# Projections in fours, one evacuation of two value banks, earlier expert rows and a spaced closing in a conv, attention and mixture-of-experts kernel

## The chip, the cores and the metric

The kernel runs on one core of a Trainium2 chip. The metric is the device time of one execution in microseconds; the time before is 1307.98 us, the median of 3 runs (1307.3 to 1308.54). A profiled execution takes longer: the one shown here ran 1332.96 us, and its trace spans 1331.2 us, with a mean granted TensorE clock of 0.989.

Engines are named as the profile names them: PE (TensorE, matmuls), PEld (its weight loads), DVE (VectorE), ACT (ScalarE), POOL (GpSimd) and SP (SyncE, which issues most DMAs). Every engine takes its own instructions in program order.

## The reference

The input is two images of 256 channels and 56 x 56 = 3136 positions, all in float32. Two layers follow each other:

```python
# layer 0: non-local block, 8 groups of 16 channels, no softmax
f = einsum('bgdn,bgdm->bgnm', theta(x), phi(x)) / n
y = einsum('bgnm,bgdm->bgdn', f, g(x))
x = relu(batch_norm(w_out @ y + b_out) + x)

# layer 1: tokens t of shape (2, 3136, 256)
q, k, v = split(ln(t) @ W_attn)                 # 4 heads of 64, causal softmax
t = t + (softmax(mask(q @ k.T / 8)) @ v) @ W_proj
probs = softmax(ln(t) @ gate_w + gate_b)        # 8 experts, each token takes 2
t = t + sum over the 2 experts of p_e * (gelu(ln(t) @ W1[e] + b1[e]) @ W2[e] + b2[e])
```

The output is t, brought back to the image layout.

## The kernel before

The kernel folds layer 0 into one matrix per image, then runs attention image by image (b = 0, 1), and then the experts. Tokens are sorted by expert into blocks of 128 rows ("slots") in DRAM, so each block is a small dense network. The engines' program order is written by hand. Background work is kept in generators, and a part of it is emitted ("pulled") between attention steps or expert blocks.

Attention goes over seven query blocks of W = 448 columns, two pairs of heads (hp) and key tiles of 128. One step is one `scores` and one `values`, three steps apart. The matmuls work on 64x64 tiles of the array, four at a time:

```python
LAG = 3
for n in range(len(steps) + LAG):
    if n < len(steps):
        ...
        between(i, ends[i] - n)             # background work of this step
    late = n >= LAG and steps[n - LAG][3]   # first values of a block
    if n >= LAG:
        due(clock[0])                       # tasks whose time has come
        clock[0] += 1
    if n >= LAG and not late:
        values(n - LAG)
    if n < len(steps):
        scores(n)
    if late:
        values(n - LAG)
```

`scores` writes exponentials into a tile `st` (a pool of 5), and DVE adds them into `acc`, for the softmax's sums:

```python
nc.scalar.activation(st[:k, :, c0:], ps[:k, :, c0:W], AF.Exp, scale=SCALE)    # L661
...
nc.vector.tensor_tensor(acc, acc, st, ALU.add)                                # L675
```

`values` accumulates into two PSUM banks, one for each half of a key tile's 128 rows. The tile that holds them, `yp`, has one buffer (`py`, bufs=1). At the end of a block both banks are brought out and added:

```python
if last:
    yh = qT[:, hp, i * W : (i + 1) * W]
    nc.scalar.copy(yh, yp[:, 0, :W])                              # L703
    nc.vector.tensor_tensor(yh, yh, yp[:, 1, :W], ALU.add)        # L704
    later.append((clock[0], sum_rows, hp, i, yh))
```

Then come, by the clock, `sum_rows` (a matmul with ones, a copy, four small DMAs and a fifth), `invert` (a reciprocal on DVE, L740, and three DMAs), `scale` (a product on DVE) and `hand_on`. For the last block of all, the DMAs of these go through POOL's queue (`queue_of`).

The projections of the next tokens are cut into pieces: a Q or K piece is a 512-column product for one pair of heads (L539), a V piece is one token tile (L558), and a transpose piece (L518) makes two token tiles ready. Each writes a PSUM bank of a pool with two buffers (`pm`, tag "m"), which ACT then copies out. They use the whole 128x128 array. They are emitted by `between`:

```python
tick[0] += 1
if tick[0] % 2:
    pull(2)
    return
nb, s = (b, i + 1) if i + 1 < NB else (b + 1, 0)
if nb < B and s < NS and (nb == b or left < NCH - QB // P - 2):
    rest = max(0, upto[s] - at[nb] - 1)
    for _ in range(2 * -(-rest // max(2, left))):
        if at[nb] + 1 < upto[s]:
            step(nb)
```

After attention the experts run block by block, GB = 3 blocks to a group. The first group's rows are brought in during attention (`early_rows`); later groups are fetched six blocks ahead. For each block PE transposes the rows (L1380), multiplies them by the first weights (L1403) and, three blocks later, by the second (L1422). DVE copies the block's first weights out of the resident ones two blocks ahead (L1391) and adds the second bias (L1432). Between blocks, `meanwhile` pulls the background work; first in that queue is `closing`, which finishes the last attention block:

```python
def closing():
    while finished[B - 1][NH - 1] < N:
        clock[0] += 4
        due(clock[0])
        yield True
        yield True
    while not projected[B - 1]:
        yield False
    queue.append(judge())
    ...

def meanwhile():
    scatters = placed[1] and not sent[1]
    pull(3 if scatters or worked[0] >= MIXED else 2)
    if side and next(side[0], None) is None:
        side.popleft()
```

After it, the second image's tokens are projected out, sorted (small DVE operations) and scattered to their slots (indirect DMAs of POOL), all beside the blocks of the first image.

Of the kernel before, what the change touches and what calls it, by code (L numbers as in the profile page):

```python
# [27 lines left out]
def conv_attn_moe_kernel(  # L28
# [75 lines left out]
    MIXED = MOST0 + E  # L104
    NBLK = (2 * B * N + E * (P - 1)) // P
    GB = 3

    MAIN = NBLK - GB
    SCALE = 1.0 / HS**0.5
# [333 lines left out]
    def layer1(nm, general):  # L443

        with ExitStack() as whole:
# [170 lines left out]
            def attend(  # L616
# [63 lines left out]
                def values(n):  # L680
                    i, hp, j, first, last, order = steps[n]
                    k = chunk(j)
                    c0 = max(0, j * P - i * W)
                    sn = f"{nm}{b}_{hp}_{i}"
                    st = sts.pop(n)
                    if first:
                        yps[hp, i] = py.tile([P, 2, 512], F32, tag="y", name=f"yp_{sn}")
                    yp = yps[hp, i]

                    for h in range(0, k, HS):  # L690
                        end = last or (h and all(chunk(o) <= h for o in order[order.index(j) + 1 :]))
                        for a in range(2):
                            nc.tensor.matmul(  # L693
                                yp[a * HS : (a + 1) * HS, h // HS, c0:W],
                                v[hp][h : h + HS, j, a, :HS],
                                st[h : h + HS, a, c0:],
                                start=first,
                                stop=bool(end),
                            )
                    if last:  # L700

                        yh = qT[:, hp, i * W : (i + 1) * W]
                        nc.scalar.copy(yh, yp[:, 0, :W])  # L703
                        nc.vector.tensor_tensor(yh, yh, yp[:, 1, :W], ALU.add)  # L704
                        del yps[hp, i]
                        later.append((clock[0], sum_rows, hp, i, yh))

                def queue_of(hp, i):

                    return nc.gpsimd if (b, hp, i) == (B - 1, NH - 1, NB - 1) else nc.sync  # L710

                def sum_rows(hp, i, yh):
                    r = (b * NH + hp) * NB + i
                    sn = f"{nm}{b}_{hp}_{i}"
                    acc = accs.pop((hp, i))
                    sp = bank(f"sp_{b}_{hp}_{i}")

                    flat = acc.rearrange("p a w -> p (a w)")
                    for g in range(4):
                        nc.tensor.matmul(  # L720
                            sp[g * 32 : (g + 1) * 32, : W // 2], ones[:, :32],
                            flat[:, g * W // 2 : (g + 1) * W // 2], start=True, stop=True,
                        )
                    line = fs.tile([P, W], F32, tag="rb", bufs=3, name=f"line_{sn}")
                    nc.scalar.copy(line[:, : W // 2], sp[:, : W // 2])
                    halves = sum_d[r].rearrange("a (h w) -> (a h) w", h=2)
                    for g in range(4):
                        queue_of(hp, i).dma_start(
                            out=halves[g : g + 1], in_=line[g * 32 : g * 32 + 1, : W // 2]
                        )  # L730
                    queue_of(hp, i).dma_start(
                        out=sums[:, r], in_=sum_d[r].rearrange("a (p f) -> (a p) f", p=HS)
                    )
                    later.append((clock[0] + 4, invert, hp, i, yh))

                def invert(hp, i, yh):
                    r = (b * NH + hp) * NB + i
                    sn = f"{nm}{b}_{hp}_{i}"
                    back = fs.tile([P, 2 * W // P], F32, tag="back", name=f"back_{sn}")
                    nc.vector.reciprocal(back, sums[:, r])  # L740
                    queue_of(hp, i).dma_start(
                        out=inv_d[r].rearrange("a (p f) -> (a p) f", p=HS), in_=back
                    )
                    rb = fs.tile([P, W], F32, tag="rb", bufs=3, name=f"rb_{sn}")
                    for a in range(2):
                        queue_of(hp, i).dma_start(
                            out=rb[a * HS : (a + 1) * HS], in_=inv_d[r, a].partition_broadcast(HS)
                        )
                    later.append((clock[0] + 4, lambda hp, i, yh: scale(hp, i, yh, rb), hp, i, yh))
# [551 lines left out]
            def experts(w1s, w2s, b2s, ex, es, ps6, between, need, written):  # L1301
# [4 lines left out]
                def fetch(g):  # L1306
                    s, e = g * GB, (g + 1) * GB
                    b = 0 if e <= FULL0 else 1
                    need(b)
                    if g == 0:  # L1310
                        return early_rows, None
                    f = known[b][0]
                    xb = ex.tile([P, GB, xds[b].shape[1]], F32, tag="xb", bufs=3, name=f"xb_{nm}_{g}")
                    if b:
                        at = nc.values_load_multi_w_load_instructions(
                            qblk[0:1, s - f : e - f],
                            engines=(SP,),
                            min_val=0,
                            max_val=NBLK - FULL0 - 1,
                            skip_runtime_bounds_check_because="a permutation's places",  # L1320
                        )[1]
# [52 lines left out]
                def inputs(n, group):  # L1374
                    xb, to = group
                    g = n % GB
                    rows = xb[g] if n < GB else xb[:, g, :C]
                    tp = ps6.tile([P, 512], F32, tag="tp", bufs=2, name=f"tp_{nm}_{n}")
                    for c in range(NH):
                        nc.tensor.transpose(  # L1380
# [257 lines left out]
            def tokens(b, qT, done):  # L1638
# [5 lines left out]
                if b == 0:  # L1644
# [8 lines left out]

                    while not read[B - 1]:
                        yield False
                    for n in range(0, GB, 2):
                        m = min(2, GB - n)
                        xb = bg.tile([P, 2, C], F32, tag="xn", name=f"xb_{nm}_first{n}")
                        nc.sync.dma_start(
                            out=xb[:, :m],  # L1660
                            in_=xds[0][n * P : (n + m) * P].rearrange("(n p) w -> p n w", p=P),
# [49 lines left out]
            else:  # L1711
# [27 lines left out]
                for b in range(B):  # L1739
# [5 lines left out]
                    def between(i, left):  # L1745
# [6 lines left out]
                        tick[0] += 1  # L1752
                        if tick[0] % 2:
                            pull(2)
                            return
                        nb, s = (b, i + 1) if i + 1 < NB else (b + 1, 0)

                        if nb < B and s < NS and (nb == b or left < NCH - QB // P - 2):
                            rest = max(0, upto[s] - at[nb] - 1)
                            for _ in range(2 * -(-rest // max(2, left))):  # L1760
                                if at[nb] + 1 < upto[s]:
                                    step(nb)

# [6 lines left out]
            def closing():  # L1770

                if not general:
                    while finished[B - 1][NH - 1] < N:
                        clock[0] += 4
                        due(clock[0])
                        yield True
                        yield True
                    while not projected[B - 1]:
                        yield False
                    queue.append(judge())  # L1780
# [5 lines left out]
            with ExitStack() as moe:  # L1786
# [11 lines left out]
                        )  # L1798
                for _ in load_w2(True):
                    pass  # L1800
                while len(early_rows) < GB:
                    pull()

                def need(b):
# [9 lines left out]
                    queue.appendleft(finish(1, oy, 3))  # L1814

                def meanwhile():
                    scatters = placed[1] and not sent[1]
                    pull(3 if scatters or worked[0] >= MIXED else 2)
                    if side and next(side[0], None) is None:
                        side.popleft()  # L1820

# [179 lines left out]
```

## Time and profile before

| What | us |
|---|---|
| median time | 1307.98 |
| profiled span | 1331.2 |
| PE busy | 1276.9 |
| DVE busy | 787.7 |
| ACT busy | 602.2 |
| POOL busy | 306.2 |
| last attention product ends, experts begin, about | 887 |
| last expert product ends, about | 1310.7 |

The page gives for each engine its busy time, its share of the span and its instructions. Busy time of PE is modelled from pipelined matmuls, and a float32 matmul counts as two instructions. The chain of work follows the end back, step by step, to what released it; its shares by engine say which engine set the time. A row of groups reads: line, engine, operation, tiles, shapes and count, then busy time and mean of one in ns, then the idle time just before them with what ended it. A row of waits reads: who waited, for whom, the sum in us, the number of times, the longest. A timeline row reads: start and length in us, engine, line, operation, tiles, count, and in brackets the idle time before with its releaser. Times in windows are from the span's start.

### The profile page before, as it was taken

The page shows a single profiled execution, that of the slowest core. Times are in us where ns is not written, and L with a number is a line of the kernel's source. Part 1 is how long each engine was busy: PE and PEld are TensorE (multiplying, and loading weights), DVE is VectorE, ACT ScalarE, POOL GpSimd, SP SyncE. Part 2 cuts the span into 40 slices and gives each one's busy share as a digit, 9 for nine tenths or more (in the row PEclk, how much of TensorE's full clock was granted, in tenths as well). Part 3 has the DMA queues.
Part 4 walks back from the last instruction along what each step waited for, and adds up shares of the span by engine and source line. Part 5 has one row for each costly group of instructions (what it writes and reads, how often), then busy time and mean ns, then how long its engine had stood idle before and what let it go on. Part 6 is the DMA issues. An engine that isn't in the chain of part 4 may idle for free.

```text
span 1331.2 us, 28014 instructions
## 1 busy us (share of the span) xinstructions
PE 1276.9 (96%) x10569; PEld 808.0 (61%) x10569; DVE 787.7 (59%) x1683; ACT 602.2 (45%) x1226; POOL 306.2 (23%) x297
## 2 busy tenths in 40 slices
PE   8999999999999999999999989989999999899995
PEld 7875444444444444444345434449988999899894
DVE  1582555748777654675768777765744443355553
ACT  0145554555565554455553455553423333244341
POOL 1113110000000111110004461010066212655541
PEclk9999999999999999999999999999999999999997
DMA  9993000000000000100001126141244433556553
GB/s 311 383 326 113 16 24 24 24 16 24 9 17 17 17 2 9 40 9 15 9 8 60 60 80 198 33 138 56 67 144 129 130 109 97 179 175 202 180 156 107
DMA packets 110471, 123.54 MB, mean 93 GB/s; under 512 B 19904, under 2 KB 100045, under 8 KB 110329
## 3 DMA queue, kind: packets, MB, share of 16 engines
q1 hardware_dynamic: 96232, 92.49, 22.4%
q0 software_dynamic: 10272, 26.00, 5.8%
q10 hardware_dynamic: 3824, 3.18, 0.8%
q8 instruction: 87, 1.43, 0.5%
q14 instruction: 56, 0.45, 0.1%
HBM read 62.65 MB, written 60.41 MB: 92 GB/s over the span
## 4 chain that ended last, share of the span: by engine, by line
PE 91%; DVE 3%; issue 2%; ACT 1%; DMA 1%; POOL 0%; DVEq 0%; SPq 0%; POOLq 0%; ACTq 0%
PE yp_f L693 20%; PE sc_f L653 19%; PE ht_f L1403 14%; PE yp_f L1422 13%; PE qk_f L539 7%; PE v_f L558 4%; PE pp_f L602 4%; PE cp L324 3%; PE gram L255 3%; PE tp_f L1380 2%; DVE acc_f L675 1%; ACT st_f L661 1%; PE sp_f L720 1%; PE yo_f L1549 1%; PE xp_f L518 1%
## 5 line engine op out<-in xcount | busy, mean ns | idle before, releaser
L661 ACT ACTIVATE st_f<-sc_f 128x896 f32<-128x896 f32 (+5 forms) x400 | 333.5, 838 | 300.1 <-PE sc_f L653 273.7
L675 DVE TENSOR_TENSOR acc_f<-acc_f,st_f 128x896 f32<-128x896 f32 (+5 forms) x372 | 366.5, 985 | 168.3 <-ACT st_f L661 161.3
L693 PE MATMUL yp_f<-st_f,v_f 64*64 64x448 f32 (+6 forms) x3184 | 340.5, 503 | 9.7 <-DVE qT_f L704 6.5
L653 PE MATMUL sc_f<-qT_f,kT_f 64*64 64x448 f32 (+6 forms) x3184 | 341.5, 500 | 4.0 <-ACT st_f L661 4.0
L1412 ACT ACTIVATE g_f<-ht_f,b1b 128x128 f32<-128x128 f32 x408 | 116.8, 371 | 243.0 <-PE ht_f L1403 127.6
L1403 PE MATMUL ht_f<-xT_f,w_f 128*128 128x128 f32 x1632 | 203.4, 277 | 9.3 <-issue 6.6
L653 PEld LDWEIGHTS sc_f<-qT_f,kT_f 64*64 64x64 f32 x3184 | 116.6, 133 | 156.4 <-issue 134.5
L693 PEld LDWEIGHTS yp_f<-st_f,v_f 64*64 64x64 f32 x3184 | 112.3, 133 | 162.6 <-issue 134.7
L1403 PEld LDWEIGHTS ht_f<-xT_f,w_f 128*128 128x128 f32 x1632 | 198.5, 193 | 14.9 <-issue 10.4
L501 POOL TENSOR_SCALAR xn_f<-t 128x256 f32<-128x256 f32 (+1 forms) x50 | 68.2, 1373 | 542.6 <-issue 330.8
L1284 POOL DMA_INDIRECT x_slots<-xr_f,idx x100 | 113.0, 1130 | 218.7 <-DVE xr_f L1276 116.6
L1391 DVE COPY w_f<-w1s_f 128x1024 f32 x102 | 71.1, 698 | 86.8 <-PE ht_f L1403 38.8
L539 PE MATMUL qk_f<-px_f,wat 128*128 128x512 f32 (+1 forms) x224 | 92.6, 558 | 1.2 <-ACT px_f L524 1.2
L1439 POOL DMA_INDIRECT y_tokens<-ys_f,to_f x60 | 60.3, 1005 | 139.7 <-DVE ys_f L1432 109.8
L1432 DVE TENSOR_TENSOR ys_f<-yp_f,kT_f 128x128 f32<-128x128 f32 x102 | 29.6, 291 | 99.7 <-PE yp_f L1422 65.3
L663 DVE TENSOR_TENSOR st_f<-st_f,keep 128x256 f32<-128x256 f32 (+1 forms) x112 | 44.2, 395 | 68.2 <-ACT st_f L661 67.7
L539 PEld LDWEIGHTS qk_f<-px_f,wat 128*128 128x128 f32 x224 | 38.7, 190 | 54.4 <-issue 45.3
L1422 PE MATMUL yp_f<-px_f,g_f 128*128 x204 | 62.7, 390 | 1.0 <-issue 1.0
L1422 PE MATMUL yp_f<-v_f,g_f 128*128 x204 | 61.5, 382 | 0.8 <-issue 0.8
L1422 PE MATMUL yp_f<-kT_f,g_f 128*128 x204 | 62.1, 386 | 0.0
L1422 PE MATMUL yp_f<-w2s_f,g_f 128*128 x204 | 61.2, 382 | 0.3 <-issue 0.3
L1496 POOL DMA_INDIRECT y_f<-y_slots,idx x50 | 54.8, 1096 | 16.3 <-issue 14.7
(259 smaller groups left out, 1170.8 us busy)
## 6 DMA issues: line engine op xcount, KB each, us to landing
x_slots<-fill SPq DMA_DIRECT2D x1, 8127.0 KB
xb_f<-x_slots SPq DMA_DIRECT2D x60, 129.0 KB
x_slots<-fill SPq DMA_DIRECT2D x1, 7296.0 KB
y_slots<-ys_f SPq DMA_DIRECT2D x57, 128.0 KB
kept<-t SPq DMA_DIRECT2D x2, 3200.0 KB
x<-in_x_dram SPq DMA_DIRECT2D x14, 448.0 KB
xr<-in_x_rows_dram SPq DMA_DIRECT2D x12, 512.0 KB
out_dram<-ot_f SPq DMA_DIRECT2D x24, 256.0 KB
```

Of the source, the lines that this page charges most:

```text
L501: nc.gpsimd.tensor_scalar(xn[:k, a], ts[b][:k, n + a, :C], ts[b][:k, n + a, MEAN : MEAN + 1], ts[b][:k, n + a, RSTD : RSTD + 1], ALU.subtr ...
L539: nc.tensor.matmul(ps[:, :w], wat[:, c, d0 : d0 + P], xT[:, c, :w], start=(c == 0), stop=(c == NH - 1),)
L653: nc.tensor.matmul(ps[h : h + HS, a, c0:W], kT[hp][rows, j * P + h : j * P + h + HS], qT[rows, hp, q0 + c0 : q0 + W], start=True, stop=True,)
L661: nc.scalar.activation(st[:k, :, c0:], ps[:k, :, c0:W], AF.Exp, scale=SCALE)
L675: nc.vector.tensor_tensor(acc[:k, :, c0:], acc[:k, :, c0:], st[:k, :, c0:], ALU.add)
L693: nc.tensor.matmul(yp[a * HS : (a + 1) * HS, h // HS, c0:W], v[hp][h : h + HS, j, a, :HS], st[h : h + HS, a, c0:], start=first, stop=bool( ...
L1284: s = nc.gpsimd.indirect_dma_start(out=xds[b], out_offset=bass.IndirectOffsetOnAxis(ap=idxs[b][:kk, k, n : n + 1], axis=0), in_=xr[:kk], i ...
L1391: nc.vector.tensor_copy(w, w1s[:, :, bass.ds(e, 1), :].rearrange("p c e h -> p c (e h)"))
L1403: nc.tensor.matmul(ht[:, k, :], w[:, c, k * P : (k + 1) * P], xT[:, c, :], start=(c == 0), stop=(c == NH - 1),)
L1412: nc.scalar.activation(g[:, k, :], ht[:, k, :], AF.Gelu, bias=b1bs[b][:, k, i : i + 1])
L1422: nc.tensor.matmul(yp[:, :C], g[:, k, :], w2s[k][:, bass.ds(e, 1), :].rearrange("p e d -> p (e d)"), start=(k == 0), stop=(k == KH - 1),)
L1439: s = nc.gpsimd.indirect_dma_start(out=y_tokens, out_offset=bass.IndirectOffsetOnAxis(ap=to[:, n % GB : n % GB + 1], axis=0), in_=ys, in_o ...
```

## The change

It has five parts.

- **Projections.** Background projections are emitted on every fourth attention step and no longer on every second, four pieces at a time and no longer two. It is for fewer changes between the 64x64 tiles of attention and the whole array.
- **Value banks.** ACT copies both banks into a scratch tile from the exponentials' pool, and POOL adds the halves. It is for releasing the banks after one operation.
- **Expert rows.** The rows of the first two groups, six blocks, are brought in during attention, two of them in tiles of another tag.
- **Closing.** The tasks of the last attention block are spaced by three and then two expert blocks, where it was one each, and their DMAs go through SP's queue. It is for not letting DVE's queue stand before a DMA.
- **Sorting.** From the moment the second image is projected until it is scattered, three background pieces are pulled per expert block; before, that was so only for the scatters.

```diff
+    EARLY = 2
...
-                        nc.scalar.copy(yh, yp[:, 0, :W])
-                        nc.vector.tensor_tensor(yh, yh, yp[:, 1, :W], ALU.add)
+                        both = fst.tile([P, 2, W], F32, tag="st", name=f"both_{sn}")
+                        nc.scalar.copy(both, yp[:, :, :W])
+                        nc.gpsimd.tensor_tensor(yh, both[:, 0], both[:, 1], ALU.add)
...
-                def queue_of(hp, i):
-
-                    return nc.gpsimd if (b, hp, i) == (B - 1, NH - 1, NB - 1) else nc.sync
...                       (its four uses become nc.sync)
-                    if g == 0:
-                        return early_rows, None
+                    if g < EARLY:
+                        return early_rows[s:e], None
...
-                    rows = xb[g] if n < GB else xb[:, g, :C]
+                    rows = xb[g] if n < EARLY * GB else xb[:, g, :C]
...
-                    for n in range(0, GB, 2):
-                        m = min(2, GB - n)
-                        xb = bg.tile([P, 2, C], F32, tag="xn", name=f"xb_{nm}_first{n}")
+                    for n, m in ((0, 2), (2, 2), (4, 1), (5, 1)):
+                        name = f"xb_{nm}_first{n}"
+                        if m == 2:
+                            xb = bg.tile([P, 2, C], F32, tag="xn", name=name)
+                        else:
+                            xb = bg.tile([P, C], F32, tag="xr", name=name).unsqueeze(1)
...
+                        if tick[0] % 4:
                             return
...
-                            for _ in range(2 * -(-rest // max(2, left))):
+                            for _ in range(4 * -(-rest // max(4, left))):
...
+                    blocks = deque((3, 2))
                     while finished[B - 1][NH - 1] < N:
                         clock[0] += 4
                         due(clock[0])
-                        yield True
-                        yield True
+                        for _ in range(2 * blocks.popleft() if blocks else 0):
+                            yield True
...
-                while len(early_rows) < GB:
+                while len(early_rows) < EARLY * GB:
...
-                    scatters = placed[1] and not sent[1]
-                    pull(3 if scatters or worked[0] >= MIXED else 2)
+                    sorting = projected[1] and not sent[1]
+                    pull(3 if sorting or worked[0] >= MIXED else 2)
```

In `between` only odd ticks pull, as before; the projections' part is now reached by every fourth tick alone. Cuts in the diff and in the code are marked with three dots.

More of the change, by code (lines that the diff above doesn't have):

```diff
@@ L727, in sum_rows @@
                     for g in range(4):
-                        queue_of(hp, i).dma_start(
+                        nc.sync.dma_start(
                             out=halves[g : g + 1], in_=line[g * 32 : g * 32 + 1, : W // 2]
                         )
-                    queue_of(hp, i).dma_start(
+                    nc.sync.dma_start(
                         out=sums[:, r], in_=sum_d[r].rearrange("a (p f) -> (a p) f", p=HS)
@@ L740, in invert @@
                     nc.vector.reciprocal(back, sums[:, r])
-                    queue_of(hp, i).dma_start(
+                    nc.sync.dma_start(
                         out=inv_d[r].rearrange("a (p f) -> (a p) f", p=HS), in_=back
@@ L745, in invert @@
                     for a in range(2):
-                        queue_of(hp, i).dma_start(
+                        nc.sync.dma_start(
                             out=rb[a * HS : (a + 1) * HS], in_=inv_d[r, a].partition_broadcast(HS)
```

## The prediction

> **What bounds the kernel now.** I read the page from the top: busy shares, then the chain of work that ended last, then the waits of the matmul engine alone, and last the timeline wherever a wait was long.
>
> ```profile
> span 1331.2 us, 28014 instructions
> ...
> PE 1276.9 (96%) x10569; PEld 808.0 (61%) x10569; DVE 787.7 (59%) x1683; ACT 602.2 (45%) x1226; POOL 306.2 (23%) x297
> ...
> PE 91%; DVE 3%; issue 2%; ACT 1%; DMA 1%; POOL 0%; DVEq 0%; SPq 0%; POOLq 0%; ACTq 0%
> ```
>
> PE is busy 96% of the span and is 91% of the chain. No other engine is above 59%. So a change can gain only in two ways: by filling some of the 1331.2 - 1276.9 = 54.3 us in which PE is idle, or by making its busy time shorter for the same arithmetic. The arithmetic is the same before and after. Of the idle time, 6.2 us is the first load and about 15 us lies after 1300 us (14.37 + 1.69 us busy of 31.2); the change reaches neither. The profiled span is 1331.2 us and the timed median 1307.98, so I scale profile microseconds by 0.983 at the end.
>
> The busy time hides a cost. In the timeline of PE in mid-attention, `sc_f` and `yp_f` are the two attention products and `v_f` a projection piece (columns: start, us, then the group):
>
> ```profile
> 289.52 0.93 PE L653 MATMUL sc_f<-qT_f,kT_f 64*64 64x448 f32 x8
> 290.38 2.05 PE L558 MATMUL v_f<-wv,px_f 128*128 128x264 f32 x8
> 292.36 0.98 PE L693 MATMUL yp_f<-st_f,v_f 64*64 64x448 f32 x8
> 293.16 0.93 PE L653 MATMUL sc_f<-qT_f,kT_f 64*64 64x448 f32 x8
> 293.91 0.93 PE L693 MATMUL yp_f<-st_f,v_f 64*64 64x448 f32 x8
> 294.66 0.93 PE L653 MATMUL sc_f<-qT_f,kT_f 64*64 64x448 f32 x8
> 295.52 1.16 PE L558 MATMUL v_f<-wv,px_f 128*128 128x264 f32 x4
> 296.61 0.98 PE L693 MATMUL yp_f<-st_f,v_f 64*64 64x448 f32 x8
> 297.42 0.93 PE L653 MATMUL sc_f<-qT_f,kT_f 64*64 64x448 f32 x8
> ```
>
> Start to start, an undisturbed step (scores at 293.16 to 294.66) takes 1.50 us. With one V tile in it (294.66 to 297.42) it takes 2.76, that is 1.26 more; with two (289.52 to 293.16) it takes 3.64, that is 2.14 more. A second V tile costs 0.88 us, so the first one's other 0.38 us is the price of going from 64x64 tiles to the full array and back. It is counted as busy.
>
> Real waits of PE that the change touches, from its waits, the DVE timeline and the PE timeline:
>
> ```profile
> PE yp_f L693 <- DVE qT_f L704: 6.5, 6, 1.5
> ```
> ```profile
> 897.51 0.20 DVE L740 RECIPROCAL back_f<-sums 128x7 f32<-128x7 f32 x1 [6.50 <-DMA sums<-sums]
> 897.70 0.69 DVE L1391 COPY w_f<-w1s_f 128x1024 f32 x1
> ```
> ```profile
> 893.43 0.41 PE L1380 MATMUL tp_f<-ident,xb_f 128*128 128x128 f32 x2 [1.15 <-DMA xb_f<-x_slots]
> ...
> 898.54 2.99 PE L1403 MATMUL ht_f<-xT_f,w_f 128*128 128x128 f32 x16 [2.69 <-DVE w_f L1391]
> ```
>
> The first: the value bank (one buffer) is released only when DVE has added its second half. The others: at the start of the experts DVE stands for 6.50 us before a small reciprocal whose sums are still in a DMA; the weight copy behind it comes late, and PE stands for 2.69 us. Just before, PE waits 1.15 us for expert rows.
>
> **What the Trainium skill says.** "TensorEngine Tiling (Array Packing)", Key Properties: changing the tiling mode drains the TensorE. The trace agrees, with the 0.38 us above per excursion. "SBUF — State Buffer", Who interferes with whom: a VectorE instruction with two SBUF inputs contends with a GpSimd instruction that reads SBUF, and the second to start blocks. The new GpSimd add reads SBUF, and the attention sums (L675) have two SBUF inputs; no run here shows it yet. "GPSIMD Engine Reference", Engine selection: GpSimd is about 2x slower than VectorE for two inputs. No such GpSimd row exists before. "TensorE: Matmul & The Clock Gate", HAM oscillation: idle gaps throttle the array's clock. The trace agrees: after the 2.69 us wait the 16 matmuls at 898.54 take 2.99 us against a usual 1.95.
>
> **The change part by part.**
>
> Projections four at a time. Comparing the two programs' PE order from the first attention product to the last, attention is interrupted 99 times before and 72 times after (groups with projections in them: 58 and 33). So 27 excursions vanish: 27 x 0.38 = 10.3 us of PE time. Against it: the projections write through two PSUM buffers, emptied by ACT. Four Q or K pieces run at about 1.75 us each, and a copy takes 0.53, so they need not wait. Groups "V, transpose, V, V" are tighter: the third piece needs the first one's bank, and ACT still has an exponential (0.92) ahead of it. I estimate ready time: the exponential ends 1.17 us after the group's start, two V copies (0.27 each) end near 1.8, and PE wants the bank at about 1.4. So 0.4 us; 8 such groups plus those in the two long clumps at the second query block: about 10 x 0.4 = 4 us lost. Net gain 6.3 us.
>
> One copy for both banks. Removed: 28 ACT copies of 448 (527 ns) and 28 DVE adds (615 ns, 17.2 us). Added: 28 ACT copies of 896. From the copy rows, 132 columns take 271 ns and 512 take 532, but the exponential of 896 takes 0.92 us; I take 0.87. Also 28 GpSimd adds of 448 columns: twice DVE's 0.62 is 1.2 us; scaling the normalisation row (1373 ns for 256) gives 2.4 us; 35 to 67 us in all, beside PE. The release of the bank now follows one ACT copy, not copy, DVE queue and add. In the wait at 517.56 the copy ran at 515.55 and the add ended at 517.51; a 0.87 us copy would have ended at 516.42, so that 1.49 us wait shrinks by about 1.1. Of the 6.5 us I keep 5. One more stop of 1.41 us at 778.82, put down to "issue", followed the same add, which stood behind a scatter's DVE work; I count 1 of it. Gain 6 us. The new scratch tile is taken from the exponentials' five buffers. At a block's end four are held, so it fits, if GpSimd finishes within about four steps (6 us).
>
> Early expert rows. The 1.15 us wait goes: its rows are loaded in attention, and the next group is needed three blocks later. Gain 1.1 us.
>
> Spaced closing. The reciprocal now stands behind five weight copies and not three. From the order, that is after the third hidden block; the sums' DMAs go through the sync queue and have three blocks. Even if they land a little late, the delayed copy is for a block that starts later. So the 2.69 us go, and with them the slow clock: 2.99 - 1.95 = 1.0 us in that group, and about 0.7 more in the transposes and outputs after it (outputs 2.20 against 1.73 in the chain). Gain 4.4 us. The b=1 sort starts some two blocks later but runs at three pieces per block; in the order its last scatter comes slightly earlier, so the second half of the experts does not wait.
>
> Sum: 6.3 + 6 + 1.1 + 4.4 = 17.8 us of the profile, 17.5 us timed: 1307.98 - 17.5 = about **1290.5 us**.
>
> **The rivals.** (1) The bank wait eats the switching gain: four pieces at two buffers make PE wait for ACT in most groups. For: ACT is the only way out. Against: the one clump of V, transpose, V, V in the trace (505.76 to 509.42) shows only about 0.26 us at the third piece. If it cost the whole 10.3 us: 1297. (2) GpSimd becomes a bound: its in-order queue holds the add behind scatters of about 1 us each, and DVE is locked out during adds; exponentials then wait for a buffer. For: POOL is 14.72 of 20 us busy at 760 to 780 us. Against: most of attention has it idle, and DVE has slack and loses 17 us of adds. At 1 us for each of 28 block ends it would take 28 us and make 1318. I give that little weight. (3) DVE in the sorting stretch: three pieces a block. At 920 to 940 DVE is busy 13.65 of 20 us at two pieces; 1.26 us a block is weights and outputs, leaving 1.3 for two pieces, so three make about 3.2 of 3.73 us. It fits, but a row of long pieces may hold PE: 2 to 4 us. (4) Stops put down to "issue" (992 to 999, 1020 to 1025, 1142 to 1147, 1163 to 1166 us) have no named releaser; they may move by some microseconds either way.
>
> **Range and chances.** If rival 1 takes all of the switching and rival 3 comes true: 1300. If there are no bank waits and two of the stops vanish: 1282. Beyond 2% (under 1281.8) needs 26 us, nearly all idle time the change can touch: chance 0.1. Slower by over 2% needs rival 2 in full: 0.01.
>
> **What would show each step.** PE busy total should fall by about 8 us, mostly as shorter excursions. A four-piece Q/K group should take about 7.1 us in one run and a lone scores step stay 1.50. The PE wait for the bank should be under 2 us, now behind ACT. No DVE wait on the sums over 2 us with PE waiting after it. GpSimd adds of 1.2 to 2.4 us. I am wrong if PE waits for projection copies by over 5 us, if exponentials wait for GpSimd, or if PE's "issue" stops grow.

## The result, and the profile after

The changed kernel took **1301.65 us** (median of 4 runs) beside 1308.26 us for the kernel before (4 runs): a ratio of 0.9947, 95% interval 0.993 to 0.9964. That is 6.6 us faster; 17.5 were predicted, so the time lies just outside the predicted range of 1282 to 1300.

One thing about the comparison comes first. Chips differ: over six groups of runs the kernel before took 1307.5 to 1308.5 us on three and 1334.3 to 1337.0 us on the other three, and the changed kernel moved with it. Below, chips of the first kind are called A and of the second B (theories A and B in the expectations are something else), and times are only compared within one group. Each chip was used in one group only, so the chip and the time at which it was used are not told apart. The trace that the prediction was read from (1332.96 us) is like B in its span and in its stops; the times stated before are like A. Its profile was not slower because it was profiled, as the first part of this document says: on an A chip the profiled execution of the kernel before took 1308.1 us.

So the page of the kernel before is shown again, from an A chip, and then that of the changed kernel:

```profile
span 1306.4 us, 28014 instructions
...
PE 1267.3 (97%) x10569; PEld 803.3 (61%) x10569; DVE 791.3 (61%) x1683; ACT 602.8 (46%) x1226; POOL 308.4 (24%) x297
```
```profile
span 1299.4 us, 28014 instructions
...
PE 1263.0 (97%) x10569; PEld 805.6 (62%) x10569; DVE 791.9 (61%) x1655; ACT 610.4 (47%) x1226; POOL 346.4 (27%) x317
```

PE busy falls by 4.3 us, where about 8 were predicted, and its idle time from 39.1 to 36.4. The waits of PE say more. First the kernel before on the A chip, then the changed kernel (who waited, for whom, sum in us, times, longest):

```profile
PE yp_f L693 <- DVE qT_f L704: 8.1, 7, 1.5
...
PE ht_f L1403 <- DVE w_f L1391: 2.8, 1, 2.8
...
PE tp_f L1380 <- DMA xb_f<-x_slots: 1.4, 1, 1.4
```
```profile
...
PE sc_f L654 <- ACT st_f L662: 2.3, 4, 0.6
PE qk_f L540 <- ACT px_f L525: 2.2, 2, 1.2
...
PE v_f L559 <- ACT v_f L568: 0.7, 3, 0.3
...
PE qk_f L540 <- ACT qT_f L548: 0.5, 2, 0.3
```

All three waits that the change was aimed at are gone: 8.1 + 2.8 + 1.4 = 12.3 us. In their place stand scores that wait for an exponential and projections that wait for ACT's copies (1.2 us of the second row, before the first scores, were there before too). By stage, from the two PE timelines of one A chip (the kernel before, and the changed kernel run beside it, span 1299.5):

| stage | before | after | difference |
|---|---|---|---|
| until the first scores | 109.3 | 109.9 | +0.6 |
| attention, first to last scores | 769.0 | 764.6 | -4.4 |
| experts, first transposes to the last product's end | 406.7 | 402.8 | -3.9 |
| after the last product | 19.1 | 19.9 | +0.8 |

The 2.3 us between the last scores and the experts are the same in both. The prediction had 12.3 us for attention and 5.5 for the experts. Most of what is missing is missing in attention.

### The profile page after: what moved, and what is told of

Same layout as the page of the kernel before. It is cut to its first block, busy times and chain, and to the rows that moved or that the text cites. A ratio compares the mean times of both kernels' runs of the same rounds, so it can differ in the third digit from the quotient of the medians.

```text
span 1299.4 us, 28014 instructions
## 1 busy us (share of the span) xinstructions
PE 1263.0 (97%) x10569; PEld 805.6 (62%) x10569; DVE 791.9 (61%) x1655; ACT 610.4 (47%) x1226; POOL 346.4 (27%) x317
## 4 chain that ended last, share of the span: by engine, by line
PE 79%; issue 7%; DMA 5%; DVE 5%; ACT 3%; POOL 1%; DVEq 0%; SPq 0%; POOLq 0%; ACTq 0%
PE yp_f L694 16%; PE sc_f L654 16%; PE ht_f L1401 13%; PE yp_f L1420 12%; PE qk_f L540 6%; PE cp L325 3%; PE v_f L559 3%; PE pp_f L603 3%; PE gram L256 3%; DVE acc_f L676 2%; PE tp_f L1378 2%; ACT st_f L662 1%; DMA kept<-t 1%; DMA y_tokens<-ys_f,to_f 1%; PE sp_f L718 1%
## 5 line engine op out<-in xcount | busy, mean ns | idle before, releaser
L676 DVE TENSOR_TENSOR acc_f<-acc_f,st_f 128x896 f32<-128x896 f32 (+5 forms) x372 | 377.8, 1016 | 162.1 <-ACT st_f L662 153.3
L1401 PE MATMUL ht_f<-xT_f,w_f 128*128 128x128 f32 x1632 | 199.5, 275 | 0.6 <-ACT xT_f L1382 0.6
L706 POOL TENSOR_TENSOR qT_f<-both_f 128x448 f32<-128x448 f32 x28 | 37.2, 1328 | 522.1 <-ACT both_f L705 522.1
L502 POOL TENSOR_SCALAR xn_f<-t 128x256 f32<-128x256 f32 (+1 forms) x50 | 74.5, 1498 | 139.4 <-DVE t L171 47.7
```

The source lines that it names most:

```text
L502: nc.gpsimd.tensor_scalar(xn[:k, a], ts[b][:k, n + a, :C], ts[b][:k, n + a, MEAN : MEAN + 1], ts[b][:k, n + a, RSTD : RSTD + 1], ALU.subtr ...
L676: nc.vector.tensor_tensor(acc[:k, :, c0:], acc[:k, :, c0:], st[:k, :, c0:], ALU.add)
L1401: nc.tensor.matmul(ht[:, k, :], w[:, c, k * P : (k + 1) * P], xT[:, c, :], start=(c == 0), stop=(c == NH - 1),)
```

## The experiments

### The parts alone (B chip: 1337.03 us for the kernel before)

The kernel before, once more, for its profile:

> The kernel before, unchanged, profiled once more. Theory A (the trace that the prediction was read from was an unusual execution): its span was 1331.2 us while timed runs took 1308, so about 23 us of its stops are not in a usual run; a second trace should span about 1306 to 1310 us, without the stops put down to issue at 992 to 999, 1020 to 1025, 1142 to 1147 and 1163 to 1166 us. Theory B (profiling itself slows this kernel by 1.7%, as the prediction assumed): again about 1331 us, with the same stops.

It took 1334.36 us, and PE again had stops that no engine explains:

```profile
PE ht_f L1403 <- issue: 6.4, 11, 1.1
```

Then the fours alone, the banks alone, and the three experts' parts (early rows, closing, sorting) alone:

```diff
fours:  +                        if tick[0] % 4:
                                     return
        -  range(2 * -(-rest // max(2, left)))
        +  range(4 * -(-rest // max(4, left)))
banks:  -  nc.scalar.copy(yh, yp[:, 0, :W])
        -  nc.vector.tensor_tensor(yh, yh, yp[:, 1, :W], ALU.add)
        +  both = fst.tile([P, 2, W], F32, tag="st", ...)
        +  nc.scalar.copy(both, yp[:, :, :W])
        +  nc.gpsimd.tensor_tensor(yh, both[:, 0], both[:, 1], ALU.add)
```

> Only the projections in fours on every fourth step; value banks, expert rows, closing and sorting as before. The prediction's terms: 27 excursions at 0.38 us less 4 us of waits for ACT, 6.3 us faster (1302). Rival 1 (waits for the two PSUM buffers eat it): 0 to 2 us. If waits are nearly absent, as the trace of the whole change suggests (PE waits behind projection copies about 3.5 us against 2.5 before): 9 us.

> Only the one ACT copy of both value banks and the GpSimd add. The prediction: 6 us faster. Theory A: the waits for the bank (6.5 us in 6 places) are in a usual run too, so about 5 us. Rival 2 (GpSimd adds block DVE or are late, exponentials wait): same or slower.

> Only early expert rows, spaced closing with its DMAs on the sync queue, and three pieces a block while sorting; attention as before. The prediction: 5.5 us faster (1.1 rows, 4.4 closing). Theory A: the 6.5 us stand of DVE may be shorter in a usual run, so 2 to 5 us. Rival 3 (sorting at three pieces makes PE wait for DVE): 0 or slower.

The fours alone took 1345.31 us, **8.3 us slower** (ratio 1.0071, 1.0053 to 1.009). The banks alone took 1332.85, 4.2 us faster (0.9971, 0.9961 to 0.9981). The experts' parts alone: 1336.94, nothing (0.9997, 0.9986 to 1.0008). The parts alone add up to 4 us slower; the whole was faster. So the parts are not independent.

### One part taken back at a time (A chip: 1307.49 us)

The changed kernel again, then without the fours, then without the banks, then fours and banks without the experts' parts; the edits are those above, reversed.

> The changed kernel as it is, on the same chip as the other runs of this call, so that the whole change can be set beside its parts. On the chip of the first experiments the kernel before took 1337.0 us. Theory A (the parts help each other: the bank change takes away a wait that the fours bring out): 6 to 14 us faster than the kernel before on this chip, more than the 4 us that the parts made alone. Theory B (the parts add up: +4.2 us for the banks, +0.1 for the experts' parts, -8.3 for the fours): 4 us slower, as far as the chip stays the same. In either case I look at whether stops of PE put down to 'issue' are there in the experts, as in the kernel before, or gone, as in the first profile of the changed kernel.

> The changed kernel with projections in twos on every second step as before; banks, early rows, closing and sorting as changed. Theory A: the fours are worth a gain once the banks are changed, so this is 2 to 8 us slower than the changed kernel. Theory B (fours cost 8 us whatever stands beside them): this is about 8 us faster than the changed kernel, and about 4 us faster than the kernel before.

> The changed kernel with the two value banks copied and added by ACT and DVE as before; fours, early rows, closing and sorting as changed. Theory A: like the fours alone, some 8 us slower than the kernel before, with PE waiting about 13 us for DVE's add at the block ends. Theory B: the same 8 us slower, but then the changed kernel must be only 4 us faster than this. The distance to the changed kernel tells: A 14 us or more, B 4 us.

> The kernel before with the fours and the bank change together, without early rows, closing and sorting. Theory A: 5 to 12 us faster than the kernel before, and within 2 us of the changed kernel, as the experts' parts alone gave nothing (ratio 0.9997). Theory B: 4 us slower than before. If it lies more than 3 us above the changed kernel, the experts' parts gain only when the earlier stages run in the new order.

| kernel | us | ratio to before | interval |
|---|---|---|---|
| changed | 1301.87 | 0.9957 | 0.9944 to 0.9971 |
| changed, without fours | 1302.74 | 0.9965 | 0.9952 to 0.9979 |
| changed, without banks | 1313.12 | 1.0041 | 1.0028 to 1.0055 |
| fours and banks only | 1304.49 | 0.9976 | 0.9967 to 0.9986 |

The theory of parts that help each other (A in the expectations) holds in its direction: taking the banks back costs 11.2 us and makes the kernel slower than before; added alone they were worth 4.2. Its numbers were too high throughout: 5.6 us for the whole where it had 6 to 14, 0.9 for taking back the fours (2 to 8), 11.2 for the banks (14 or more), 3.0 for fours and banks (5 to 12). With the banks in place the fours are worth 0.9 us, which these intervals don't tell from nothing; without them they cost 8 on the B chip. The profile shows why. Without the bank change, PE's waits for DVE's add are, with the fours:

```profile
PE yp_f L694 <- DVE qT_f L705: 12.9, 10, 2.4
```

The kernel before has 6 or 7 such waits with 6.5 to 8.1 us. The fours add three or four block ends at which no projection group stands between the last value product of one block and the first of the next. At about 174 and 564 us, for example, the kernel before has a Q/K group there, over the copy and the add; with the fours it comes some microseconds earlier, and PE waits 0.68 and 2.07 us. In the changed kernel there is still no group at these places, and a small wait is left that the records don't name: ACT's copy of both banks ends at 176.75 us and the next value products begin at 176.81, 0.35 us late; the same 0.35 us stands at 154 and 564 us.

The saving itself is measured from the PE timeline. The extra time of a group is the start of the attention group after it (less the wait before that), minus the start of the one ahead of it, minus that one's usual 0.75 us:

| group | extra us | kernel |
|---|---|---|
| two Q/K pieces | 3.74 | without fours |
| four Q/K pieces | 7.17 | changed |
| V, V | 2.09 | without fours |
| transpose, V | 1.59 | without fours |
| V, transpose, V, V | 3.78 | changed |

Four Q/K pieces save 2 x 3.74 - 7.17 = 0.31 us. The measure leaves out that the second attention group after any projection group begins 0.05 us late (0.80 us after the first, and not 0.75); with it, as the prediction counted over a whole step, the saving is 0.36 us. A V group saves nothing: 3.78 against 2.09 + 1.59 = 3.68. In the changed kernel's PE timeline one V group looks like this; the wait in the third row is what eats the switch:

```profile
286.07 1.16 PE L559 MATMUL v_f<-wv,px_f 128*128 128x264 f32 x4
287.16 0.33 PE L519 MATMUL xp_f<-ident,xn_f 64*128 64x64 f32 x2
287.76 2.05 PE L559 MATMUL v_f<-wv,px_f 128*128 128x264 f32 x8 [0.27 <-ACT v_f L568]
```

In groups with a full transpose (229 and 613 us) no wait is recorded, but the turn is the same: the third piece begins at 230.44 us, 0.05 us after ACT's copy of the first ends. Q/K groups ran as predicted, 7.13 us with no wait:

```profile
272.32 7.13 PE L540 MATMUL qk_f<-px_f,wat 128*128 128x512 f32 x16
```

### The group moved, and the banks once more (B chip: 1334.32 us)

```diff
-                        between(i, ends[i] - n)      # ahead of values
...
                     if n < len(steps):
+                        between(i, ends[i] - n)      # between values and scores
                         scores(n)
```

> The kernel before, for its profile on the chip of this call. The trace that the prediction was read from spans 1331.2 us, while the timed runs took 1308. Theory P (profiling costs 1.7%, as the prediction assumed): the profiled execution takes 1330 us or more here too, although the changed kernel's profiled execution took no longer than its timed ones. Theory C (that trace is of a chip that stops PE and ACT for reasons the profile does not show): on a chip where the kernel before is timed at 1307 the profile spans 1304 to 1308 us, the waits put down to 'issue' in the experts (6.4 us of the first expert product on the other chip) are under 1 us, and the experts take about 405 us and not 424 to 427.

> The changed kernel with the projection groups emitted between values and scores, where they stood between scores and values. So ACT has the last exponential 0.75 us earlier and should be free for the first V copy. If the V groups lose their switching gain to the copy behind an exponential (a group of V, transpose, V, V takes 3.78 us, the same three V and one transpose in two groups 3.68): the group falls to 3.4 us, some ten groups give 3 to 4 us, the waits of scores for exponentials (2.2 us) fall too, and the time is 2 to 5 us under the changed kernel. If two buffers are too few however ACT is ordered: the group stays at 3.7 to 3.8 us and the time within 1 us.

> The changed kernel once more, so that the moved groups and the bank change alone have it beside them on one chip. About 5.6 us under the kernel before (ratio 0.9957 and 0.9947 so far), if the chip is like the last one; on a chip like the first one the parts' sum is open.

> The bank change alone, once more. On the first chip it was worth 4.2 us (ratio 0.9971), though the wait that it takes away measured 6.5 us. If the rest went into waits for the normalised rows that GpSimd makes (2.2 us): here too 3 to 4.5 us under before, and in the trace the transposes wait about 2 us for xn. If the first chip's stops had a part in it: 1.5 to 3 us (before minus the changed kernel without the fours is 4.75, of which the experts' parts are about 2.6).

The profiled execution of the kernel before took 1339.26 us on this B chip, so it could not decide between the theories. The changed kernel took **1331.21** us here, 0.998 of before (0.9968 to 0.9992): the 30 us come with the chip in both kernels. Moving the groups did not help: 1333.5 us, 0.9993 (0.9979 to 1.0007). The V group stayed at 3.78 us though ACT was now idle ahead of its copy. PE, then ACT, in the kernel with the groups moved:

```profile
286.97 1.16 PE L559 MATMUL v_f<-wv,px_f 128*128 128x264 f32 x4
288.06 0.33 PE L519 MATMUL xp_f<-ident,xn_f 64*128 64x64 f32 x2
288.66 2.05 PE L559 MATMUL v_f<-wv,px_f 128*128 128x264 f32 x8 [0.27 <-ACT v_f L568]
```
```profile
286.36 0.92 ACT L662 ACTIVATE st_f<-sc_f 128x896 f32<-128x896 f32 x1 [0.59 <-PE sc_f L654]
288.17 0.44 ACT L568 COPY v_f<-v_f 128x132 f32<-128x132 f32 x2 [0.89 <-PE v_f L559]
```

ACT stands idle for 0.89 us until the V product ends, and PE still waits 0.27. So the wait is not the exponential ahead of the copy, as the prediction had it. It is the turn of two buffers: the third piece needs the first one's bank, and between them lie only a short transpose and 0.44 us of copies. The prediction had the size right (0.4 us a group) for the wrong reason.

The banks alone gave 1331.21 us, 0.9978 (0.9967 to 0.9989): 3.1 us, after 4.2 on the first B chip. On this chip the other four parts added nothing to them. On both, PE had a wait that neither the kernel before nor the changed one has:

```profile
PE xp_f L518 <- POOL xn_f L501: 2.2, 2, 1.2
```

These are transposes that wait for the second image's first normalised rows. POOL's timeline tells why. In the kernel before (A chip) POOL makes these rows as soon as it has nothing else to do:

```profile
286.06 2.87 POOL L501 TENSOR_SCALAR xn_f<-t 128x256 f32<-128x256 f32 x2 [44.95 <-PE xp_f L518]
453.26 5.15 POOL L501 TENSOR_SCALAR xn_f<-t 128x256 f32<-128x256 f32 x4 [164.33 <-issue]
```

Changed, without the fours (A chip):

```profile
446.44 1.25 POOL L706 TENSOR_TENSOR qT_f<-both_f 128x448 f32<-128x448 f32 x1 [39.15 <-ACT both_f L705]
447.68 11.28 POOL L502 TENSOR_SCALAR xn_f<-t 128x256 f32<-128x256 f32 x8
```

Before, the first pair was ready at 289 us, some 160 us early. The new add stands in the same in-order queue at every block end and holds POOL in step with attention; at 447.68 it has to make four pairs in a row, and PE overtakes it. In this trace the array is also slow after the two waits, at a granted clock of 0.52 from 454 to 456 us: of the next groups of attention products, two took 1.77 and 1.50 us where 0.93 is usual, 1.4 us more.

```profile
454.81 1.77 PE L694 MATMUL yp_f<-st_f,v_f 64*64 64x448 f32 x8
456.36 1.50 PE L654 MATMUL sc_f<-qT_f,kT_f 64*64 64x448 f32 x8
```

So this takes back 2.2 + 1.4 = 3.6 us here. The slow clock does not follow always: the same two waits, 1.16 and 1.01 us, stand in four traces. In two (this one and the second of the banks alone) the clock fell; in the first of the banks alone, and in the next section's with Q and K alone in fours, it stayed at 1.00, the groups took 0.93 to 0.98 us, and only the 2.2 us are lost.

### Q and K alone in fours, and the closing taken back (A chip: 1308.51 us)

```diff
+  size = 4 if the next piece is Q or K else 2        (in words)
-  if tick[0] % 4: return
+  if tick[0] % size: return
-  range(4 * -(-rest // max(4, left)))
+  range(size * -(-rest // max(size, left)))
```

> The kernel before, for its profile. If the chip is one on which it is timed at 1307: span 1304 to 1308 us, attention about 772 to 774 us from the first to the last score, experts 405 to 408 us, no stops put down to 'issue' of over 1 us in all, the waits for DVE's add 6.5 to 8 us. If the chip is like the other ones: 1333 to 1339 us, and nothing new.

> The changed kernel with Q and K pieces four at a time on every fourth step, V and transpose pieces two at a time on every second, as in the kernel before. A Q/K group of four saves 0.31 us against two groups of two (7.17 against 7.48 us), a V group of four loses 0.1 us (3.78 against 3.68) and makes exponentials wait. If that is where the gain was lost: 1 to 4 us faster than the changed kernel. If the waits for exponentials (1.4 us) come from the Q/K groups: within 1 us of the changed kernel.

> The changed kernel with the closing's tasks one block apart, their DMAs through GpSimd's queue, and the sort at two pieces, all as before; fours, banks and six early blocks as changed. If the closing is worth what was predicted (4.4 us): 3 to 5 us slower than the changed kernel, with PE waiting 2 to 4 us for the weight copy. If it is worth little because the sums' DMA mostly lands in time: within 1.5 us, and the rest of the 2.6 us is the early rows'.

> The changed kernel on this chip: ratio to the kernel before of 0.995 to 0.996 if the chip is one of 1307 us for the kernel before, 0.998 if it is one of 1334 us.

The kernel before took 1308.1 us under the profiler: the page shown at the start. It has no stops put down to "issue" in the experts, and takes 406.7 us there (the changed kernel 402 to 403), against 425 to 432 us in the three B traces of the kernel before. So theory C of the expectation above, of a chip that stops PE, holds. With Q and K alone in fours: 1302.41 us, 0.9958 (0.9944 to 0.9972), beside 1301.25 for the changed kernel (0.9948, 0.9934 to 0.9962). No gain. The projection groups did get shorter, 152.9 us in all against 154.2, though they now hold the 2.2 us for the rows, which were back, and scores waited longer for exponentials:

```profile
PE sc_f L654 <- ACT st_f L662: 3.1, 4, 1.3
...
PE xp_f L519 <- POOL xn_f L502: 2.2, 2, 1.2
```

Without the closing and the sorting: 1303.42 us, 0.996 (0.9946 to 0.9973), 2.2 us above the changed kernel, between the two expectations, and the wait for the weight copy is back in the profile:

```profile
PE ht_f L1405 <- DVE w_f L1393: 2.5, 1, 2.5
```

### The add on DVE (B chip: 1334.39 us)

```diff
-  nc.gpsimd.tensor_tensor(yh, both[:, 0], both[:, 1], ALU.add)
+  nc.vector.tensor_tensor(yh, both[:, 0], both[:, 1], ALU.add)
```

> The changed kernel with the halves of the value banks added by DVE out of the scratch tile, where GpSimd adds them. The banks' release is the same ACT copy. If GpSimd's add costs nothing on the path (in the changed kernel no transpose waits for rows): within 1 us of the changed kernel (ratio to before 0.994 to 0.9957). If DVE's queue was what held things up: slower by 1 us or more. The running sums (1016 ns beside GpSimd's adds, 985 without) should fall to 985.

> Q and K in fours, V in twos, and the add on DVE. If GpSimd's adds delay the normalised rows: the 2.2 us wait of the transposes goes, and it is 1.5 to 2.5 us faster than with the add on GpSimd (ratio to before about 0.994). If the rows are late because PE is earlier: the wait stays and the ratio is 0.9958 as before.

In the changed kernel it made 1339.68 us, 1.0035 (1.0022 to 1.0047), where the changed kernel itself had 0.998 on a B chip. With Q and K alone in fours it made 1337.25, 1.0014 (1.0002 to 1.0027). The wait for the rows was indeed gone in the latter, so POOL's add is what delays them. But it gained nothing: attention took 770.7 us in it, the changed kernel 770.5 on the other B chip. In both, scores waited 4.7 us for exponentials, where the changed kernel on a B chip had 3.6. A reading that fits, but is not shown: the scratch tile is one of the exponentials' buffers, and DVE's queue gives it back late. The running sums fell to 986 ns as expected. No version tried beats the changed kernel.

## Why the prediction was wrong

**Bound and aims: right.** PE stayed at 97% of the span, and each wait named went away. A four-piece Q/K group took 7.13 us (7.1 predicted), a lone scores step stayed 1.50, POOL's add took 1.25 us (1.2 to 2.4 predicted). ACT's copy of both banks took 0.90 us for 0.87:

```profile
L705 ACT COPY both_f<-yp_f x28: 900/902/911, 129.8 to 876.8; 128x896 f32<-128x896 f32 x28
L706 POOL TENSOR_TENSOR qT_f<-both_f x28: 1129/1245/1726, 130.8 to 877.8; 128x448 f32<-128x448 f32 x28
```

(The three figures are the shortest, median and longest in ns.)

**The step that failed: "Sum: 6.3 + 6 + 1.1 + 4.4".** The prediction added 6.3 us for the fours and 6 for the banks, as if each acted on an otherwise unchanged kernel. Both together measured 1307.49 - 1304.49 = 3.0 us, and the fours alone cost 8.3: the groups whose switches they saved had covered the banks' release, and PE's waits for the add went from 6.7 to 13.2 us in that pair of traces. From the A traces, taking the changed kernel without the fours as the step between:

| attention, us | before | banks, no fours | changed |
|---|---|---|---|
| length | 769.0 | 766.8 | 764.6 |
| PE waits for the value banks | 8.1 | 0.9 | 0.2 |
| transposes behind POOL's rows | 0 | 2.2 | 0 |
| scores behind exponentials | 0 | 0.9 | 2.3 |
| projections behind ACT's copies or DVE | 0 | 0 | 2.9 |
| the rest | 1.9 | 2.8 | 2.5 |
| all waits | 10.0 | 6.7 | 7.9 |
| length less waits | 759.0 | 760.1 | 756.7 |

(The rest are mostly values behind exponentials; in the middle column also 0.7 us of the sums' products behind the projections' copies.)

- *Banks, "Gain 6 us".* The recorded bank waits fell by 7.2 us, so the mechanism and its size were right. The length fell by only 2.2: other waits took back 3.9 (7.2 less the 3.3 by which all waits fell), and slow matmuls after the rows' wait 1.4. Rival 2 had looked at scatters and DVE being locked out; it missed that POOL's work had been running ahead and no longer could.
- *Rival 2 came true once, at small cost.* One of the 28 block ends falls among the scatters. There ACT's copy ends at 771.13 us, but in POOL's queue the add stands behind a running scatter and three more, about 1 us each, and runs at 775.21; an exponential waits 3.18 us for its tile, and scores 0.62 us for the exponential (the kernel before waited 1.41 us for the add there). All seven A traces with the add on GpSimd show this wait of 3.2 us. POOL, ACT and PE of the changed kernel:

```profile
775.21 1.15 POOL L706 TENSOR_TENSOR qT_f<-both_f 128x448 f32<-128x448 f32 x1
```
```profile
776.39 1.73 ACT L662 ACTIVATE st_f<-sc_f 128x896 f32<-128x896 f32 x2 [3.18 <-POOL qT_f L706]
```
```profile
777.37 0.98 PE L654 MATMUL sc_f<-qT_f,kT_f 64*64 64x448 f32 x8 [0.62 <-ACT st_f L662]
```

- *Fours, "27 x 0.38 = 10.3".* The price of one excursion was nearly right, 0.36 us by the Q/K groups; 27 x 0.36 = 9.7. The loss at V groups, about 0.4 each, was right in size and wrong in cause. That would leave 5.7 where 6.3 was put. By the lengths less waits, 760.1 - 756.7 = 3.4, of which the slow matmuls are 1.4, the switching gave 2.0. Of the difference about 1 us are the three unrecorded waits of 0.35 us for ACT's copy at the block ends that lost their group; the rest is not located. The recorded waits rose by 1.2 us: 1.4 more of scores behind exponentials and 2.9 of projections behind copies and DVE, against 2.2 that the rows' wait no longer costs, because the group with the transposes begins two steps later.
- *The counter-check caught little.* Of the signs listed as failure, two (over 5 us behind projection copies, growing "issue" stops) stayed away, and the third, an exponential held by POOL, came at one place. PE busy fell by 4.3 us and not by 8. The loss came in waits of 0.2 to 1.2 us in several places, most of them not on the list.

**Early rows and closing: right where they act, smaller in the end.** From the start of the experts to the first output products, the kernel before took 15.2 us and the changed one 10.1: 5.1 saved, 5.5 predicted. With the closing taken back it took 14.4, so 0.8 belong to the early rows (1.1 predicted) and 4.3 to the closing (4.4). Here is the end of that stretch, before (A chip) and after:

```profile
887.12 0.41 PE L1380 MATMUL tp_f<-ident,xb_f 128*128 128x128 f32 x2 [1.36 <-DMA xb_f<-x_slots]
...
892.34 3.23 PE L1403 MATMUL ht_f<-xT_f,w_f 128*128 128x128 f32 x16 [2.81 <-DVE w_f L1391]
```
```profile
882.91 2.05 PE L1401 MATMUL ht_f<-xT_f,w_f 128*128 128x128 f32 x16 [0.60 <-ACT xT_f L1382]
...
885.02 1.95 PE L1401 MATMUL ht_f<-xT_f,w_f 128*128 128x128 f32 x16
```

Over the whole of the experts 3.9 us are left. On the A chip the changed kernel has one more wait, 1.0 us at 1142 us, of an output transpose for its sum; the rest of the 1.2 us given back is not located. Another 0.8 us is lost after the last product. In timed runs the two parts are worth 2.6 us (1304.49 - 1301.87) and the closing with the sorting 2.2 (1303.42 - 1301.25), where the intervals of the compared ratios still overlap; on a B chip they were worth nothing, though in its trace this stretch went from 14.5 to 9.2 us as well. The 0.4 us that would remain for the early rows is below what these runs resolve. Rival 3 did not come true: at 920 to 940 us DVE was busy 18.02 of 20 us in the changed kernel, and PE 19.82.

**The scale and the trace.** The factor 0.983 changed the sum by 0.3 us only. The premise, that profiling slows the kernel, was wrong, though, and two readings with it: the stops put down to "issue" (rival 4) belong to B chips and are in no A trace; and the stop of 1.41 us at 778.82, also put down to "issue", is one more wait for DVE's add in the A trace, 7 times and 8.1 us for 6 times and 6.5.

**What stays open.** Why B chips stop PE: on one, the changed kernel's PE waits 10.1 us put down to "issue" for its expert products, and is busy 1276.4 us instead of 1263. Why the same two waits slow the array in two traces and not in two others. And whether making the second image's first rows ahead of POOL's adds would free the 2.2 us of waits in a kernel with Q and K alone in fours: it was not tried.

## What to carry to other kernels

Two savings on the same engine are not added until it is known what lay under what: a group that costs a switch may be hiding a buffer's release, so fewer groups bring more waits to light, and here the fours alone lost 8 us that the bank change had first to win back. Before moving an operation to an idle engine, look at what that engine does early in its queue; idle time there may be work that has run ahead, and an operation tied to another engine's progress stops that. And read the trace from a chip on which the kernel takes the time that is to be improved.

## What the runs showed of the hardware

- The same kernel takes 1308 us on some chips and 1334 to 1337 on others, at a mean granted TensorE clock of 0.993 and 0.986. Attention differs by 4.5 to 6 us, the experts by 19 to 25, of which about 10 us are stops of PE without a releaser in the trace.
- A GpSimd addition of two SBUF operands of 128x448 in float32 took 1.245 us; DVE needed 0.618 for the same one. The factor of about 2 that the prediction took from its page held.
- With the adds on GpSimd the running sums on DVE took 1016 ns in the mean and not 986, and 986 again with the add on DVE. The mean hides where it falls: the median stayed (1.091 and 1.092 us), but a full-width sum that starts while an add runs took 1.4 to 1.8 us, as below in the changed kernel. The runs agree with the Trainium skill, "SBUF — State Buffer", Who interferes with whom: the one that starts second is held. The normalising operations on GpSimd went from 1371 to 1485 ns.

```profile
215.69 1.39 POOL L706 TENSOR_TENSOR qT_f<-both_f 128x448 f32<-128x448 f32 x1 [17.69 <-ACT both_f L705]
```
```profile
216.47 1.56 DVE L676 TENSOR_TENSOR acc_f<-acc_f,st_f 128x896 f32<-128x896 f32 x1 [0.38 <-ACT st_f L662]
```

- Two waits of 1.16 and 1.01 us within 2.6 us were followed by two groups of attention products at about half speed in two traces, and by none in two others. The section of the Trainium skill that the prediction names, "TensorE: Matmul & The Clock Gate", HAM oscillation, speaks of idle gaps over about 3.4 us; these, and the 2.69 us of the prediction, were shorter.
